# Layer 2 of a four-layer graph kernel: where its weights and sums are computed

## The chip, the cores and the metric

The kernel runs on one core of a Trainium2 chip. A core has five engines that run their own instruction streams side by side: TensorE (PE in the profile; its loads of stationary operands are PEld), VectorE (DVE), ScalarE (ACT), GpSimd (POOL) and SyncE (SP), which here issues the large loads. The metric is the device time of one execution in microseconds (us), the median of several runs.

## The reference

Four graph layers follow one another, each added to its input and normalised row by row. x has 4096 rows of 64 numbers, and adj is a 4096 x 4096 matrix of zeros and ones in f32 (64 MB), read by every layer. Layer 2 is the one that matters here:

```python
support = input @ weight
mask = (adj != 0).astype(support.dtype)
rank = jnp.cumsum(mask, axis=1)
deg = rank[:, -1:]
k = jnp.minimum(deg, float(MAX_NEIGH))      # MAX_NEIGH = 100
pos = rank - (deg - k)
w = mask * jnp.where(pos > 0, DECAY ** (k - pos), 0.0)   # DECAY = 0.5
out = w @ support + bias
```

Of each row's edges, the last one counts with weight 1, the one before it with 1/2, then 1/4, and so on. An edge's weight is therefore 2 to the power of minus the number of edges behind it in its row. Layers 1 and 3 are hyperbolic attention layers with a sum over all pairs of rows, and layer 0 is a mean over neighbours.

## The kernel before

**Tiling.** The rows i of adj are split into four groups s of 1024 (WW), worked on in the order 3, 2, 1, 0. The columns j are split into 32 blocks of 128, from the last to the first. One load (`load`, issued by SyncE) brings two blocks of one group, g = j // 2, as 1 MB of f32. The pool of loads has six buffers. Blocks lie on the partitions, rows i along the free dimension. The upper 16 bits of each f32 are read in place as bf16.

**Counting (`count`, matmul at L1569).** For every row the number of edges behind the current block is kept in PSUM, in a tile z that lives for the whole pass. Two matmuls per 512 rows bring it up to date for a block: `pass_by` times the edges of the previous block, then `enter` times the edges of this one. Afterwards z holds, for each j of the block and each row i, the number of edges behind j, less 255 if (j, i) is an edge. A z is thus counted into, read, and counted into again, block after block.

**Weights (`weights_of`, L1576).** ScalarE computes 2 to the power of minus (z + 282) from PSUM into a bf16 tile, with Exp: about nothing where there is no edge. A factor of 2 to the 27 is put back with the bias (L1494).

**Sums (`add_up`, L1581).** The supports are held as a sum of two f16 halves, high and low, in `halves[:, j]`, 128 columns wide. Four matmuls per group and block multiply the high and the low 64 columns with the two times 512 rows of weights. The two row halves go to the upper and the lower 64 partitions of one accumulator, so two such matmuls, each 64 columns wide, lie side by side in the array.

**Passes.** Groups 3 and 2 go together through the *wide pass*: z tiles of 128 x 1024, two of them. Groups 1 and 0 each have a *narrow pass*, in which the two z tiles are the two halves of 512 rows. Sums run one block behind the weights (`lag`). At the end of a pass ScalarE copies the accumulator (L1610), and `end_2` turns it back to rows with four transposes (L1095).

**Row work.** Normalising, preparing layer 3 and finishing layer 1 are written as generators that `tick` steps forward between blocks: small operations on VectorE and GpSimd, some casts, copies and logarithms on ScalarE, transposes on TensorE. In the wide pass the supports of the lower groups must be ready before their blocks come (`need`), and the pass pauses for them.

**Order.** Inside the layer-2 section `manual_schedule(engines=FIXED)` holds TensorE and ScalarE to the order in which the code is written. A planner orders VectorE's instructions. VectorE also holds, for every odd g, a check that adj contains only zeros and ones (`check`, L838): one instruction over the whole 1 MB load, which needs that load and nothing else. Layer 3 follows outside that section, and three of its sigmoids (L1074) were placed by the planner inside the last narrow pass, where ScalarE changes its function table before and after each.

Lines that the prediction names: L1569 counts; L1576 weights; L1581 sums; L838 check; L1080, L1082, L1077 the pair work of layers 1 and 3; L1494 to L1504 the first row work after a pass, L896 the product y that the casts L899 to L901 wait for; L947 copies, L950 logarithms of `prepare`.

Of the kernel before, what the change touches and what calls it, by code (L numbers as in the profile page):

```python
# [10 lines left out]
F32 = mybir.dt.float32  # L11
F16 = mybir.dt.float16
I32 = mybir.dt.int32
BF16 = mybir.dt.bfloat16
AF = mybir.ActivationFunctionType
ALU = mybir.AluOpType
# [3 lines left out]
P = 128  # L20
N = 4096
D = 64
NB = N // P
W = 512
NS = N // W
SB = W // P
# [3 lines left out]
WW = 1024  # L30
# [20 lines left out]
LN2 = 0.6931471805599453  # L51
OFF_EDGE = 255.0
CUT = 27.0
SUP = 512.0
SUP_TOP = 120.0

# [2 lines left out]
def gnn_stack_kernel(  # L59
# [15 lines left out]
    nc = tc.nc  # L75
    V = nc.vector
# [3 lines left out]
    ident = const.tile([P, P], F32, name="ident")  # L80
# [488 lines left out]
    def stream(fits):  # L569

        with ExitStack() as st:
# [69 lines left out]
            def need(tag):  # L641
                while tag not in done:
                    assert queues[0] or queues[1], tag
                    tick(1)
# [446 lines left out]
            def to_rows_of(sums):  # L1091

                t = take(F32, P, SB, 2, D)
                for k in range(SB):
                    nc.tensor.transpose(t[:, k], sums[:, k * P : (k + 1) * P], ident)  # L1095
                return t.rearrange("p k h f -> p h k f")
# [185 lines left out]
            enter = keep.tile([P, P], BF16, name="enter")  # L1282
            pass_by = keep.tile([P, P], BF16, name="pass_by")
            edge_of = keep.tile([P, P], BF16, name="edge_of")
            V.tensor_scalar(edge_of, ident, OFF_EDGE, None, ALU.mult)
            V.memset(pass_by, 1.0)
            nc.gpsimd.affine_select(
                out=enter, in_=pass_by, compare_op=ALU.is_gt, fill=0.0, base=0,
                pattern=[[-1, P]], channel_multiplier=1,
            )  # L1290
            V.tensor_sub(enter, enter, edge_of)
            V.tensor_sub(pass_by, pass_by, enter)
            at_edge = num(keep, "at_edge", 1)
            V.memset(at_edge, -(OFF_EDGE + CUT) * LN2)


            w2_twice = keep.tile([P, D], F32, name="w2_twice")
# [190 lines left out]
            def end_2(s, sums):  # L1488
                z = grp("z0")
                yield 1  # L1490
                yield from free()
                t = to_rows_of(sums)
                yield 1
                V.scalar_tensor_tensor(  # L1494
                    z.rearrange("p (h k) f -> p h k f", h=2)[:, 0], t[:, 0], 2.0**CUT / SUP,
                    b2_sb[:, None, :].to_broadcast([P, SB, D]), ALU.mult, ALU.add,
                )
                V.scalar_tensor_tensor(
                    z.rearrange("p (h k) f -> p h k f", h=2)[:, 1], t[:, 1], 2.0**CUT / SUP,
                    b2_sb[:, None, :].to_broadcast([P, SB, D]), ALU.mult, ALU.add,  # L1500
                )
                held.pop()
                yield 1
                V.tensor_add(z, z, x_of(2)[:, blocks(s), :])  # L1504
                yield 1
                yield from norm_rows(3, s, z, x2[:, blocks(s)])
                yield from prepare(3, s, att3, batt3_sb, curve3, 1e-30, good[:, 1], 40)

            def wide_pass(two):

                zs = [z_tile() for _ in two]

                accs = [ps.tile([P, W], F32, name="acc"), third_z[:, :W]]
                behind, lag = [None, None], []
                for g in reversed(range(NB // 2)):
                    edges = [load_2(s, g) for s in two]
                    need((2, 2 * g // WB))
                    for k in (1, 0):
                        j = 2 * g + k
                        w = sb.tile([P, 2, WW], F32, name="sq").bitcast(BF16)[:, :, :WW]  # L1520
                        for i, edge in enumerate(edges):
                            here = edge[:, k * WW : (k + 1) * WW]
                            count(zs[i], behind[i], here, j, WW)
                            behind[i] = here
                            weights_of(zs[i], WW, w[:, i])
                            if i == 1:
                                for of, acc in enumerate(accs if lag else ()):
                                    add_up(acc, *lag[of])
                                lag = [(j, w[:, n, :W], w[:, n, W:]) for n in range(2)]
                            if two[0] != GROUPS[0] or j < BLOCKS[4]:  # L1530
                                tick(1)
                for of, acc in enumerate(accs):
                    add_up(acc, *lag[of])
                return accs

            def narrow_pass(s):

                zs = [z_tile() for _ in range(2)]
                acc = ps.tile([P, W], F32, name="acc")
                behind, lag = [None, None], []  # L1540
                for g in reversed(range(NB // 2)):
                    edge = load_2(s, g)
                    for k in (1, 0):
                        j = 2 * g + k
                        w = sb.tile([P, 2, WW], F32, name="sq").bitcast(BF16)[:, 0, :WW]
                        for h in range(2):
                            here = edge[:, k * WW + h * W : k * WW + (h + 1) * W]
                            count(zs[h], behind[h], here, j, W)
                            behind[h] = here
                            weights_of(zs[h], W, w[:, h * W : (h + 1) * W])  # L1550
                        if lag:
                            add_up(acc, *lag.pop(0))
                        lag.append((j, w[:, :W], w[:, W:]))
                        tick(1)
                add_up(acc, *lag.pop(0))
                return [acc]

            def load_2(s, g):
                a, edge = load(s, g)
# [11 lines left out]
                                start=j == BLOCKS[0], stop=True, skip_group_check=True,  # L1571
                            )

            def weights_of(z, n, w):

                nc.scalar.activation(w, z[:, :n], AF.Exp, bias=at_edge, scale=-LN2)  # L1576

            def add_up(acc, j, *ws):
                for part in range(2):
                    for h, w in enumerate(ws):  # L1580
                        nc.tensor.matmul(  # L1581
                            acc[h * D : (h + 1) * D, :],
                            halves[:, j, part * D : (part + 1) * D], w,
                            start=j == BLOCKS[0] and part == 0,
                            stop=j == BLOCKS[-1] and part == 1,
                        )
# [16 lines left out]
            with tc.manual_schedule(engines=FIXED):  # L1603
                spare.append(of_third)

                for some in (GROUPS[:2], GROUPS[2:3], GROUPS[3:]):
                    accs = wide_pass(some) if len(some) == 2 else narrow_pass(some[0])
                    for s, acc in zip(some, accs):
                        sums = row.tile([P, W], F32, name="sums", bufs=2)
                        nc.scalar.copy(sums, acc)  # L1610
                        later(end_2(s, sums))
                spare_ends()

# [95 lines left out]
```

## Time and profile before

| | us |
|---|---|
| median of 3 runs | 1109.06 (1108.8 to 1110.59) |
| span of the profiled execution | 1106.6 |
| own time of that execution beyond its span | not given by the page |
| layer 2, first to last count (L1569) | 514.3 to 757.5 |
| weights of layer 2 (L1576), ScalarE busy | 149.3 |
| TensorE, VectorE, ScalarE busy over the span | 1001.9, 915.5, 803.1 |
| mean of one check (L838) | 2.29 |

The profile records one execution. The span goes from its first to its last instruction; the time of the runs also holds what lies around it. A line of the timeline reads: start, duration, engine, line, operation, output <- input, partitions x elements, how many in a row, and in brackets how long the engine was idle before and what ended that. Durations of two matmuls in a row overlap, so the distance of starts is the better measure on TensorE. A line of the chain of waits names the piece of work that the end of the kernel hung on at that time. Windows give busy time by engine in a stretch. "out<-in" uses the program's tile names; an output "z" of L1581 is the second accumulator, which lies in the third z tile.

### The profile page before, as it was taken

What the parts mean: (1) busy time and instruction counts of PE and PEld (TensorE: products, weight loads), DVE (VectorE), ACT (ScalarE), POOL (GpSimd) and SP (SyncE); (2) the same over time, 40 slices, a digit from 0 to 9 for tenths busy, and PEclk for the clock granted to TensorE, in tenths of its full rate; (3) what the DMA queues carried; (4) which work ended last, traced back from release to release, by engine and by line L of the source; (5) the groups of instructions that cost most, each with busy time, mean ns of one, the idle gap of its engine ahead of it and who ended that gap; (6) DMA issues with size and microseconds to landing.
All of it is one profiled execution on the core that took longest, in us unless ns stands there. A gap on an engine that the chain in (4) does not pass through costs nothing.

```text
span 1106.6 us, 13832 instructions
## 1 busy us (share of the span) xinstructions
PE 1001.9 (91%) x4949; PEld 392.4 (35%) x4949; DVE 915.5 (83%) x1452; ACT 803.1 (73%) x892; POOL 273.1 (25%) x649
## 2 busy tenths in 40 slices
PE   4998998889999999998998998789899999999980
PEld 2454554333333333332333332223333333333320
DVE  5777977989999999999456484545999999999996
ACT  0003123879999999897676788889899998998960
POOL 0011212010144443525500010000001444346173
PEclk8999999889999999999998999799999999999995
DMA  9999999536565565654877987477545656666400
GB/s 341 378 419 380 370 423 396 190 131 244 191 240 219 188 238 219 228 194 148 333 304 275 362 289 261 155 270 285 203 169 211 251 214 229 228 227 227 164 1 23
DMA packets 38581, 271.63 MB, mean 245 GB/s; under 512 B 4710, under 2 KB 4710, under 8 KB 5734
## 3 DMA queue, kind: packets, MB, share of 16 engines
q1 hardware_dynamic: 37728, 270.03, 64.8%
q8 instruction: 41, 0.67, 0.2%
q10 hardware_dynamic: 774, 0.63, 0.2%
q14 instruction: 38, 0.31, 0.1%
HBM read 269.58 MB, written 1.05 MB: 245 GB/s over the span
## 4 chain that ended last, share of the span: by engine, by line
PE 55%; DVE 24%; ACT 9%; DMA 5%; POOL 3%; issue 2%; ACTq 0%; SPq 0%; POOLq 0%; DVEq 0%
PE acc L1037 15%; PE z L1569 9%; DVE t L1082 7%; PE z L1059 7%; PE z L1065 6%; PE z L1062 6%; DVE t L1080 6%; DMA edges<-in_adj_dram 4%; PE acc L1581 3%; PE acc L1414 3%; ACT sq L1077 3%; ACT sq L1576 2%; DVE junk L838 2%; ACT sig L1074 1%; PE z L1581 1%
## 5 line engine op out<-in xcount | busy, mean ns | idle before, releaser
L1080 DVE SCALAR_TENSOR_TENSOR t<-z,sig 128x1024 f32<-128x1024 f32 x256 | 308.8, 1217 | 13.0 <-ACT sq L1077 6.8
L1077 ACT ACTIVATE sq<-z,turn 128x1024 f32<-128x1024 f32 x256 | 277.8, 1111 | 45.1 <-PE z L1065 18.4
L1082 DVE SCALAR_TENSOR_TENSOR t<-sq,t 128x2048 f32<-128x2048 f32 x128 | 297.3, 2322 | 0.5
L1074 ACT ACTIVATE sig<-left_b,right 128x1024 f32<-128x1024 f32 x256 | 285.9, 1146 | 1.9 <-DVE t L1080 1.3
L1037 PE MATMUL acc<-t,xe 128*64 128x512 f32 x1024 | 255.2, 608 | 17.2 <-DVE t L1082 16.8
L1059 PE MATMUL z<-edges,two_i 128*128 128x512 bf16 x512 | 201.2, 393 | 7.4 <-DVE t L1080 7.4
L1065 PE MATMUL z<-dst,src 74*128 74x512 f16 x512 | 195.5, 382 | 0.0
L1062 PE MATMUL z<-lo_hi,hi_lo 128*128 128x512 f16 x512 | 194.4, 380 | 0.0
L1576 ACT ACTIVATE sq<-z,at_edge 128x512 bf16<-128x512 f32 (+1 forms) x192 | 149.3, 828 | 46.0 <-PE z L1569 43.5
L838 DVE SCALAR_TENSOR_TENSOR t<-edges 128x2048 bf16<-128x2048 f32 x32 | 73.0, 2287 | 54.2 <-DMA edges<-in_adj_dram 54.2
L1037 PEld LDWEIGHTS acc<-t,xe 128*64 128x64 f32 x1024 | 63.8, 136 | 145.6 <-issue 83.8
L1569 PE MATMUL z<-edges,pass_by 128*128 128x512 bf16 x248 | 89.5, 401 | 17.9 <-ACT sq L1576 17.8
L1414 PE MATMUL acc<-edges,first 128*128 128x512 bf16 x256 | 80.1, 394 | 17.6 <-DMA edges<-in_adj_dram 17.3
L1059 PEld LDWEIGHTS <-two_i 128*128 128x128 bf16 x512 | 50.3, 98 | 128.9 <-issue 82.3
L1569 PE MATMUL z<-edges,enter 128*128 128x512 bf16 x256 | 91.0, 398 | 0.0
L1414 PE MATMUL acc<-edges,third 128*65 128x512 bf16 x256 | 80.0, 394 | 0.0
L838 DVE SCALAR_TENSOR_TENSOR junk<-edges 128x2048 bf16<-128x2048 f32 x32 | 73.1, 2286 | 4.7 <-DMA edges<-in_adj_dram 4.4
L1065 PEld LDWEIGHTS <-src 74*128 74x128 f16 x512 | 49.2, 96 | 70.5 <-issue 8.0
L1062 PEld LDWEIGHTS <-hi_lo 128*128 128x128 f16 x512 | 50.4, 98 | 57.1 <-issue 11.7
L1581 PE MATMUL acc<-sq,halves 128*64 128x512 bf16 x384 | 62.5, 403 | 1.0 <-ACT sums L1088 0.8
L869 POOL TENSOR_TENSOR sq<-z 128x512 f32<-128x512 f32 x8 | 14.2, 1776 | 164.3 <-DVE z L868 132.2
L1133 POOL TENSOR_TENSOR w_att<-x,u 128x512 f32<-128x512 f32 x6 | 15.6, 2595 | 141.2 <-ACT u L1128 141.2
(375 smaller groups left out, 940.9 us busy)
## 6 DMA issues: line engine op xcount, KB each, us to landing
edges<-in_adj_dram SPq DMA_DIRECT2D x256, 1024.0 KB, 4.7
x<-in_x_dram SPq DMA_DIRECT2D x4, 256.0 KB
out_dram<-x ACTq DMA_DIRECT2D x2, 256.0 KB
out_dram<-x SPq DMA_DIRECT2D x2, 256.0 KB
w_sb<-in_L_gnn_W_dram ACTq DMA_DIRECT2D x1, 32.0 KB, 4.8
w_twice<-in_L_gnn_weight_dram ACTq DMA_DIRECT2D x2, 16.0 KB, 8.6
given<-in_L_gnn_b_dram ACTq DMA_DIRECT2D x1, 0.2 KB
given<-in_L_gnn_bias_dram ACTq DMA_DIRECT2D x1, 0.2 KB
```

Of the source, the lines that this page charges most:

```text
L838: V.scalar_tensor_tensor(junk, a, 0.0, a, ALU.not_equal, ALU.not_equal, accum_out=odd[:, n : n + 1])
L1037: it = nc.tensor.matmul(acc[h * D : (h + 1) * D, :], xe[:, j, :], t[:, k, h * W : (h + 1) * W], start=j == BLOCKS[0], stop=j == BLOCKS[-1],)
L1059: nc.tensor.matmul(half, two_i, edge[:, at : at + W], start=True, stop=False)
L1062: nc.tensor.matmul(half, hi_lo[:, of], lo_hi[:, to], start=False, stop=False)
L1065: last = nc.tensor.matmul(half, src[:, of], dst[:, to], start=False, stop=True)
L1074: nc.scalar.activation(sig, left_b, AF.Sigmoid, bias=right[:, j : j + 1])
L1077: nc.scalar.activation(sq[:, k], zp, AF.Square, bias=turn, scale=-1.0 / UNIT)
L1080: V.scalar_tensor_tensor(t[:, k], zp, 0.0, sig, ALU.max, ALU.mult)
L1082: V.scalar_tensor_tensor(t, sq, HIGH**2, t, ALU.add, ALU.mult)
L1414: nc.tensor.matmul(accs[h][:m], lhs[:, j, :], edge[:, at : at + W], start=j == BLOCKS[0], stop=j == BLOCKS[-1],)
L1569: nc.tensor.matmul(z[:, h : h + W], lhs, rhs[:, h : h + W], start=j == BLOCKS[0], stop=True, skip_group_check=True,)
L1576: nc.scalar.activation(w, z[:, :n], AF.Exp, bias=at_edge, scale=-LN2)
```

## The change

Four things change in layer 2.

1. *The sign and scale of z.* The count matrices are multiplied by -128, so that z holds -128 times what it held. ScalarE's Exp takes the other scale.
2. *Weights as bit patterns.* A bf16 number that is a power of two has its exponent in bits 7 and up. VectorE adds a constant to z, cuts at 0 and writes int16, which is the bf16 weight itself. It does this for the second group (wide) or second half (narrow) wherever g is even, that is for a quarter of all weights; ScalarE does the rest.
3. *Wide pass:* the weights of two blocks share one tile, and their sums are made together, after the counts of the first block of the next g.
4. *Narrow passes:* each half has its own accumulator of 128 partitions, and one matmul with all 128 columns of `halves` adds the high and the low part at once (64 partitions each). Two copies at the end, and eight matmuls with `stack` (two stacked identities) that add high and low while turning to rows.

```diff
-            V.tensor_scalar(edge_of, ident, OFF_EDGE, None, ALU.mult)
-            V.memset(pass_by, 1.0)
+            V.tensor_scalar(edge_of, ident, OFF_EDGE * STEP, None, ALU.mult)
+            V.memset(pass_by, -STEP)
...
+            stack = keep.tile([P, D], F32, name="stack")
+            V.tensor_add(stack, ident[:, :D], ident[:, D:])
...
-                t = to_rows_of(sums)
+                if len(sums) == 1:
+                    t = to_rows_of(sums[0])
+                else:
+                    t = take(F32, P, SB, 2, D)
+                    for k in range(SB):
+                        for h, of in enumerate(sums):
+                            nc.tensor.matmul(
+                                t[:, k, h], of[:, k * P : (k + 1) * P], stack,
+                                start=True, stop=True,
+                            )
+                    t = t.rearrange("p k h f -> p h k f")
...
+                    w = sb.tile([P, 2, WW], F32, name="sq").bitcast(BF16)
                     for k in (1, 0):
                         j = 2 * g + k
-                        w = sb.tile([P, 2, WW], F32, name="sq").bitcast(BF16)[:, :, :WW]
                         for i, edge in enumerate(edges):
                             here = edge[:, k * WW : (k + 1) * WW]
                             count(zs[i], behind[i], here, j, WW)
                             behind[i] = here
-                            weights_of(zs[i], WW, w[:, i])
-                            if i == 1:
-                                for of, acc in enumerate(accs if lag else ()):
-                                    add_up(acc, *lag[of])
-                                lag = [(j, w[:, n, :W], w[:, n, W:]) for n in range(2)]
+                            weights_of(
+                                zs[i], WW, w[:, i, k * WW : (k + 1) * WW], i == 1 and g % 2 == 0
+                            )
                             if two[0] != GROUPS[0] or j < BLOCKS[4]:
                                 tick(1)
-                for of, acc in enumerate(accs):
-                    add_up(acc, *lag[of])
-                return accs
+                        if k == 1:
+                            for args in lag:
+                                add_up(*args)
+                            lag = []
+                    lag = [
+                        (
+                            accs[i], 2 * g + k,
+                            w[:, i, k * WW : k * WW + W], w[:, i, k * WW + W : (k + 1) * WW],
+                        )
+                        for k in (1, 0)
+                        for i in range(2)
+                    ]
+                for args in lag:
+                    add_up(*args)
+                return [[acc] for acc in accs]
...
-                acc = ps.tile([P, W], F32, name="acc")
-                behind, lag = [None, None], []
+                accs = [ps.tile([P, W], F32, name="acc"), third_z[:, :W]]
+                behind, lag = [None, None], [None, None]
+
+                def add(h):
+                    if lag[h] is not None:
+                        j, w = lag[h]
+                        nc.tensor.matmul(
+                            accs[h], halves[:, j, :], w,
+                            start=j == BLOCKS[0], stop=j == BLOCKS[-1],
+                        )
...
-                            weights_of(zs[h], W, w[:, h * W : (h + 1) * W])
-                        if lag:
-                            add_up(acc, *lag.pop(0))
-                        lag.append((j, w[:, :W], w[:, W:]))
+                            add(h)
+                            part = w[:, h * W : (h + 1) * W]
+                            weights_of(zs[h], W, part, h == 1 and g % 2 == 0)
+                            lag[h] = (j, part)
                         tick(1)
-                add_up(acc, *lag.pop(0))
-                return [acc]
+                for h in range(2):
+                    add(h)
+                return [accs]
...
-            def weights_of(z, n, w):
-
-                nc.scalar.activation(w, z[:, :n], AF.Exp, bias=at_edge, scale=-LN2)
+            def weights_of(z, n, w, as_bits):
+
+                if as_bits:
+                    V.tensor_scalar(
+                        w.bitcast(I16), z[:, :n], STEP * (BIAS - CUT - OFF_EDGE), 0.0,
+                        ALU.add, ALU.max,
+                    )
+                else:
+                    nc.scalar.activation(
+                        w, z[:, :n], AF.Exp, bias=at_edge, scale=LN2 / STEP
+                    )
...
-                    for s, acc in zip(some, accs):
-                        sums = row.tile([P, W], F32, name="sums", bufs=2)
-                        nc.scalar.copy(sums, acc)
+                    for s, of in zip(some, accs):
+                        sums = [row.tile([P, W], F32, name="sums", bufs=2) for _ in of]
+                        for to, acc in zip(sums, of):
+                            nc.scalar.copy(to, acc)
```

More of the change, by code (lines that the diff above doesn't have):

```diff
@@ L13 @@
 I32 = mybir.dt.int32
+I16 = mybir.dt.int16
 BF16 = mybir.dt.bfloat16
@@ L53 @@
 CUT = 27.0
+STEP = 128.0
+BIAS = 127.0
 SUP = 512.0
@@ L1290, in stream @@
             )
-            V.tensor_sub(enter, enter, edge_of)
+            V.tensor_add(enter, enter, edge_of)
             V.tensor_sub(pass_by, pass_by, enter)
```

## The prediction

> **What bounds the kernel now.** I began with busy time and the table of 40 slices: TensorE is busy for 91% of the span, but that is an average over four layers. The groups place the only code that changes, the counts (L1569), weights (L1576) and sums (L1581) of layer 2, between 514 and 760 us. So I asked for busy time by stage: the steady part of the wide pass, then the two narrow passes (columns: window, length, busy time of PE, PEld, DVE, ACT, POOL, clock, DMA share, GB/s).
>
> ```profile
> PE 1001.9 (91%) x4949; PEld 392.4 (35%) x4949; DVE 915.5 (83%) x1452; ACT 803.1 (73%) x892; POOL 273.1 (25%) x649
> ...
> 526.00:565.00 39.00, 39.00 (x218) 14.23 (x215) 15.60 (x17) 27.54 (x26) 14.17 (x38) 1.00 0.91 345
> ...
> 626.00:687.00 61.00, 55.78 (x312) 18.65 (x310) 43.42 (x141) 49.45 (x79) 6.59 (x16) 0.97 0.80 293
> 687.00:760.00 73.00, 60.66 (x343) 20.21 (x340) 29.20 (x89) 65.18 (x94) 2.39 (x8) 0.91 0.64 233
> ```
>
> In the wide pass TensorE never pauses, ScalarE idles 30%, VectorE 60%. In the narrow passes TensorE and ScalarE take turns, and in the first one VectorE is 71% busy. Next, TensorE in order of time, wide pass:
>
> ```profile
> 529.08 0.62 PE L1569 MATMUL z<-edges,pass_by 128*128 128x512 bf16 x2
> 529.54 0.61 PE L1569 MATMUL z<-edges,enter 128*128 128x512 bf16 x2
> 530.00 0.61 PE L1569 MATMUL z<-edges,pass_by 128*128 128x512 bf16 x2
> 530.45 0.61 PE L1569 MATMUL z<-edges,enter 128*128 128x512 bf16 x2
> 531.00 0.62 PE L1581 MATMUL acc<-sq,halves 128*64 128x512 bf16 x4
> 531.45 0.60 PE L1581 MATMUL z<-sq,halves 128*64 128x512 bf16 x4
> 531.98 0.62 PE L1569 MATMUL z<-edges,pass_by 128*128 128x512 bf16 x2
> ```
>
> One block lasts 2.90 us: four pairs of count matmuls at 0.455 (1.82), then eight sums in two groups (0.91), with 0.09 lost where counts turn into sums and 0.08 on the way back. The third view is ScalarE's timeline, with the two places where TensorE waits for it:
>
> ```profile
> 518.29 2.12 ACT L1576 ACTIVATE sq<-z,at_edge 128x1024 bf16<-128x1024 f32 x2
> ...
> 530.26 2.12 ACT L1576 ACTIVATE sq<-z,at_edge 128x1024 bf16<-128x1024 f32 x2 [0.78 <-PE z L1569]
> ...
> 738.41 1.27 ACT L1576 ACTIVATE sq<-z,at_edge 128x512 bf16<-128x512 f32 x2
> 739.87 1.27 ACT L1576 ACTIVATE sq<-z,at_edge 128x512 bf16<-128x512 f32 x2 [0.19 <-PE z L1569]
> ```
> ```profile
> 519.46 0.61 PE L1569 MATMUL z<-edges,pass_by 128*128 128x512 bf16 x2 [0.57 <-ACT sq L1576]
> ...
> 739.16 0.39 PE L1569 MATMUL z<-edges,pass_by 128*128 128x512 bf16 x1 [0.97 <-ACT sq L1576]
> ```
>
> They give the chain that each running count z imposes, since it is counted into, read, and counted into again. Wide: count start to weights start 1.18 (529.08 to 530.26), weights start to next count 1.17 (518.29 to 519.46), together 2.35 us. Before, 2.90 of TensorE work lay around that chain, so it never showed. Narrow: 0.75 (738.41 to 739.16) plus 0.71 (to 739.87), 1.46, against a block of 1.56 (counts start at 632.59, then 634.15). Last, the chain of waits in the first narrow pass:
>
> ```profile
> 634.64 2.21 DVE t L838 x2
> ...
> 645.48 1.46 DVE y L896
> ...
> 647.48 0.61 ACT ys L900
> ```
>
> From 629 to 649 the end hangs on VectorE: row work of groups 3 and 2, two checks of 2.2 us within it, and casts on ScalarE that wait for y.
>
> [...]VectorE stood 6.79 us before the check at 560.57, which waited for its transfer, and nothing passed it.
>
> **The change, part by part.**
>
> *Two blocks' sums at once (wide).* Per load pair (two blocks, two groups) TensorE's order becomes counts, 16 sums, counts. It saves one pair of mode changes, 0.17. But the second block's counts are now followed directly by the next load pair's, with only 1.82 of work where z's chain needs 2.35. New period: counts and sums 1.82 + 1.82 + 0.17 = 3.81, plus 2.35, is 6.16. The second group's z comes back 1.18 + 2.17 (518.29 to its count at 520.46) = 3.35 after the count began, and is wanted at 2.35 + 0.91 = 3.26: 0.09 more. So 6.25 against 5.80, +0.45 each. Of 15 hand-overs, the first lies in layer 1's tail and two (at 566 and 593) in pauses for the supports: 12 x 0.45 = 5.4, less 3 x 0.17 where only the saving stays: **+4.9**. The 2 bf16 blocks now share one "sq" buffer; its reader is done a period before it is rewritten, so no wait there. Loads: 2.1 MB in 6.25 us is 336 GB/s, less than the 345 now carried.
>
> *Weights on VectorE.* Taken from ScalarE: 16 of 64 in the wide pass, 16 of 64 in each narrow one. No row of before has the operation. Bounds: 1.217 for L1080 (128x1024 from PSUM) and, between it and 0.42 of L1494 (256 wide), 0.69 for 512;[...] the lower end is ScalarE's 1.06 and 0.63. I take 1.2 and 0.69, 0.60 in a dense queue. In the wide pass it buys nothing: z of the first group stays on ScalarE and sets the chain. What is queued behind and ahead is the cost: the checks (2.29 us, one per transfer) and row work share VectorE's queue, and TensorE waits for this weight at the next count. In the wide pass the first check of a pair lands ahead of the weight that could follow it, the second about when that weight is ready (540.24, against a ready time of 539.6); placed ahead it costs 0.8 per two load pairs, 6 in all; placed behind, nothing. I take +1.
>
> *First narrow pass.* The VectorE stretch from 629 to 649 takes in six weights of 0.60, one of them in the 1.15 wait for GpSimd: **+3**, and TensorE's saving there is lost. The other 20 blocks: next item -2, and a weight behind row work (0.16 to 0.7 each) or a check, 10 x 0.3 = +3; with ScalarE's relief (below) -2: **+2** in all.
>
> *Full-width sums (narrow).* Four half-width sums and two mode changes (0.56 + 0.08) become two matmuls at 0.23, so TensorE's work is 0.94 + 0.46 = 1.40, and the chain of 1.46 takes over: -0.10 a block.
>
> *Second narrow pass.* Some 26 blocks at -0.10; six at its start stay bound by ScalarE, where three early sigmoids bring two table loads of 1.28 each. Relief: a ScalarE job (casts, copies, logarithms, sigmoids) between two blocks is 0.63 shorter wherever VectorE has the second half; some 24 such jobs in both passes, half of them in such blocks, part of it covered by transposes on TensorE: between 0 and -7, I take -2 and -3. Late weights, VectorE being 40% busy: +1.5. Together -2.6 - 3 + 1.5: **-4**.
>
> *Ends.* Each narrow group now has two copies of 0.58 instead of one, and eight small matmuls instead of four transposes of 0.16: +0.6 per group: **+1.2**. The new constants are a few operations before layer 0, under its loads[...].
>
> Sum: 4.9 + 1 + 2 - 4 + 1.2 = **+5.1 us**. The profiled execution's span is 1106.6, so 1111.7; the median of the runs is 1109.06, 2.5 above the span for what lies around it, so **1114.2**.
>
> **Rivals.** (1) *VectorE's order becomes the bound.* If the planner puts checks or row work ahead of weights wherever both are near, 48 weights at 0.5 to 0.8 late cost +24 to +38, less what is now counted (5): about 1133. For it: four checks in the narrow passes waited 1.7 to 9.6 us for a transfer with the queue shut behind them. Against: a check that lands while an odd load is worked on, as at 715.51 and 739.89, meets no VectorE weight, since only even loads have them. (2) *Faster.* Mechanism: ScalarE's relief in the narrow passes, at its full -7, with -6 from the full-width sums and VectorE never late: -13 + 1.2 + 4.9 = -7, about 1102. It decides once late weights cost less than 0.1 us a block. Against: the VectorE stretch at 629 to 649. (3) *A draw.* The narrow gains cancel the wide loss: relief as taken, late weights nothing outside that stretch: 1109. (4) That the wide stall is absent since sums still cover it: the written order excludes it, as ScalarE and TensorE are held to it there.
>
> **How the numbers follow.** Likeliest case, 1111.4 to 1120: 0.48. Rival 1, from 1120 on: 0.21. Rival 2: 0.17. Rival 3 (and 4 with it): 0.14. Within 0.2%, 2.2 us, a measurement can't be told from no change. So slower 0.69, same 0.14, faster 0.17. The range 1103 to 1129 leaves out about half of rival 1 and a third of rival 2.
>
> **What would show it.** Wide pass: TensorE pauses of about 0.5 us before every second first-group count, released by the weights on ScalarE, and load pairs 6.2 apart. If they stay 5.8 or fall to 5.63, my largest term is wrong. Narrow: blocks of 1.46 with one sum after each count; casts of group 3 starting some 3 us later after the wide pass's end than now; waits of TensorE for the VectorE weights, small against 20 us. Large ones mean rival 1; none, with ScalarE idle, rival 2.

## The result and the profile after

The changed kernel takes 1117.67 us (median of 4 runs, 1115.37 to 1119.26), the kernel before 1108.93 (4 runs, the three above and one more, 1107.51 to 1110.59): a ratio of 1.0078, 95% interval 1.0056 to 1.0101, so 8.7 us slower. The profiled execution took 1115.37 us, its span is 1113.6. Up to layer 2 it runs like the one of before: ScalarE's first weight starts at 518.34 us, for 518.29.

First the busy time on the page of the changed kernel, then its busy time by stage: the same steady stretch of the wide pass, and the two narrow passes, each from about the end of the pass before (columns: window, length, busy PE, PEld, DVE, ACT, POOL, clock, DMA share, GB/s).

```profile
PE 992.4 (89%) x4845; PEld 404.9 (36%) x4845; DVE 954.4 (86%) x1501; ACT 771.9 (69%) x846; POOL 274.0 (25%) x649
```
```profile
526.00:565.00 39.00, 35.09 (x196) 13.63 (x194) 21.85 (x23) 19.60 (x18) 14.20 (x38) 1.00 0.85 305
635.00:698.00 63.00, 50.47 (x248) 22.16 (x247) 52.88 (x158) 43.87 (x65) 9.30 (x16) 1.00 0.83 291
698.00:765.00 67.00, 54.97 (x289) 25.34 (x289) 39.11 (x100) 55.04 (x79) 3.23 (x8) 0.95 0.69 237
```

In the wide pass TensorE had been busy without a break, 39.00 of 39.00; now it stands for 3.9 us. ScalarE's 27.54 fell to 19.60 and VectorE's 15.60 rose to 21.85. In the first narrow pass VectorE is busy 84% of the time. The work moved as planned, off ScalarE, which is busy 31 us less over the span (771.9, for 803.1). The time did not follow.

TensorE in order of time, one load pair of the wide pass after (start, duration, line, operation, and in brackets the wait before it and its releaser; sums are left out between):

```profile
543.88 0.61 PE L1604 MATMUL z<-edges,pass_by 128*128 128x512 bf16 x2
544.34 0.61 PE L1604 MATMUL z<-edges,enter 128*128 128x512 bf16 x2
545.36 0.61 PE L1604 MATMUL z<-edges,pass_by 128*128 128x512 bf16 x2 [0.41 <-DVE sq L1612]
...
548.20 0.63 PE L1604 MATMUL z<-edges,pass_by 128*128 128x512 bf16 x2
...
550.48 0.61 PE L1604 MATMUL z<-edges,pass_by 128*128 128x512 bf16 x2 [0.30 <-ACT sq L1617]
```

The sums no longer lie between 548.20 and 550.48, and the chain of one z shows: 2.28 us from count to count. The profile lists 0.30 us of that as idle; by the starts TensorE loses 0.45, as the last pair of counts starts at 549.57, and 0.455 is the usual distance. Load pairs without a late VectorE weight start 6.13 us apart (550.48, 556.61), where two blocks had taken 5.80.

TensorE's waits over the wide pass, first two lines of before (514 to 628 us), then the changed kernel's (514 to 632 us) and those of both its narrow passes (632 to 770 us): sum, times, longest.

```profile
PE aux L1258 <- POOL x_hl L1253: 3.7, 2, 2.6
...
PE z L1569 <- ACT sq L1576: 1.3, 2, 0.7
```

```profile
PE aux L1261 <- POOL x_hl L1256: 7.3, 2, 6.2
PE z L1604 <- ACT sq L1617: 4.1, 13, 0.6
PE z L1604 <- DVE sq L1612: 2.6, 4, 1.5
...
PE z L1604 <- ACT sq L1617: 15.1, 10, 4.4
PE z L1604 <- DVE sq L1612: 6.8, 8, 1.9
PE z L1570 <- DVE z L1513: 1.1, 1, 1.1
```

In the wide pass there are the chain's 4.1 us, VectorE's late weights 2.6, and a third wait that the prediction's sum has no term for. It lies in the second pause for the supports, and its longest part grew from 2.6 to 6.2 us. ScalarE's timeline, of before and then of the changed kernel, tells what was late there:

```profile
592.58 2.12 ACT L1576 ACTIVATE sq<-z,at_edge 128x1024 bf16<-128x1024 f32 x2 [0.78 <-PE z L1569]
594.58 0.62 ACT L1252 CAST x_hl<-x 128x512 f16<-128x512 f32 x1
...
601.57 1.11 ACT L1576 ACTIVATE sq<-z,at_edge 128x1024 bf16<-128x1024 f32 x1 [1.18 <-PE z L1569]
```

```profile
596.44 1.11 ACT L1617 ACTIVATE sq<-z,at_edge 128x1024 bf16<-128x1024 f32 x1 [2.69 <-PE z L1604]
601.58 0.62 ACT L1255 CAST x_hl<-x 128x512 f16<-128x512 f32 x1 [4.02 <-DVE x L1221]
...
608.46 1.11 ACT L1617 ACTIVATE sq<-z,at_edge 128x1024 bf16<-128x1024 f32 x1 [1.18 <-PE z L1604]
```

The cast that feeds the supports waits 4.02 us for x, layer 1's last row result on VectorE. Before, the same cast did not wait. Between the two pauses VectorE now has four weights of 1.2 us (at 581.44, 585.09, 594.24, 597.94) within that row work. Two checks moved as well: before, they started behind x (591.44 and 593.65), and now they stand ahead of it (591.95 and 595.45). The operation that writes x starts at 600.79, for 590.83 before. Of these 10 us the cast waits 4; before, ScalarE came to the cast only 3 us after x was ready. The pause, measured between ScalarE's weights for the first group on either side, is 12.0 us after and 9.0 before.

By stage: the wide pass ends 8.75 us later than before (last copy of its first group's sums at 634.26 against 625.51); the first narrow pass takes 63.2 us against 61.3, the second 67.4 against 73.5 (each from one pass's last copy to the next). This boundary is not the same in both. One of layer 3's three early sigmoids now stands, with its table load, between the two copies that end the first narrow pass:

```profile
695.05 0.59 ACT L1654 COPY sums<-acc 128x512 f32<-128x512 f32 x1 [0.26 <-PE acc L1570]
695.66 1.28 ACT L1077 ACT_TABLE_LOAD   x1
696.95 1.15 ACT L1077 ACTIVATE sig<-left_b,right 128x1024 f32<-128x1024 f32 x1
698.01 0.57 ACT L1654 COPY sums<-z 128x512 f32<-128x512 f32 x1
```

Before, all three come after the pass's copy (687.35; the first table load is at 689.12). If these 2.4 us are counted with the second pass as before, the first takes 60.8 us and the second 69.8, which is -0.5 and -3.7. At the end of the second pass the loss is down to 4.6; what follows brings it to 7.0 in this execution.

### The profile page after: what moved, and what is told of

It reads as the page before. It is cut to its first block, busy times and chain, and to the rows that moved or that the text cites. A ratio compares the mean times of both kernels' runs of the same rounds, so it can differ in the third digit from the quotient of the medians.

```text
span 1113.6 us, 13643 instructions
## 1 busy us (share of the span) xinstructions
PE 992.4 (89%) x4845; PEld 404.9 (36%) x4845; DVE 954.4 (86%) x1501; ACT 771.9 (69%) x846; POOL 274.0 (25%) x649
## 5 line engine op out<-in xcount | busy, mean ns | idle before, releaser
L1080 ACT ACTIVATE sq<-z,turn 128x1024 f32<-128x1024 f32 x256 | 277.9, 1111 | 46.2 <-PE z L1068 19.7
L1617 ACT ACTIVATE sq<-z,at_edge 128x512 bf16<-128x512 f32 (+1 forms) x144 | 116.3, 830 | 76.4 <-PE z L1604 67.7
L1612 DVE TENSOR_SCALAR sq<-z 128x512 int16<-128x512 f32 (+1 forms) x48 | 41.6, 866 | 25.6 <-PE z L1604 17.3
```

The lines of the kernel that those rows point to most:

```text
L1080: nc.scalar.activation(sq[:, k], zp, AF.Square, bias=turn, scale=-1.0 / UNIT)
```

## The experiments

The change has three parts: A, the sums of two blocks at once in the wide pass; B, a quarter of the weights on VectorE; C, the full-width sums in the narrow passes with their two copies and the matmuls with "stack". The twelve kernels are combinations of these; two of them, e6 and e12, change the tile of the row work as well. All twelve keep the new sign and scale of z. e2, e7 and e11 have A, the others the old order of sums in the wide pass. The times below are ratios to the kernel before with their 95% intervals; a difference in microseconds is a difference of ratios times 1109, and its interval combines the two.

| run | parts | median us | ratio to before |
|---|---|---|---|
| the change | A, B, C | 1117.67 | 1.0078 (1.0056 to 1.0101) |
| e1_no_batch | B, C | 1115.57 | 1.0057 (1.0037 to 1.0076) |
| e2_no_bits | A, C | 1113.77 | 1.0040 (1.0019 to 1.0061) |
| e3_full_only | C | 1107.57 | 0.9977 (0.9960 to 0.9994) |
| e4_narrow_bits_full | C, B in both narrow passes | 1113.95 | 1.0038 (1.0020 to 1.0056) |
| e5_second_pass_bits | C, B in the second narrow pass | 1106.04 | 0.9975 (0.9959 to 0.9991) |
| e6_rows_out_of_third | e4, row work in "aux" only | 1111.19 | 1.0021 (0.9998 to 1.0043) |
| e7_batch_only | A | 1114.67 | 1.0043 (1.0028 to 1.0059) |
| e8_second_pass_bits_only | B in the second narrow pass | 1107.28 | 0.9975 (0.9957 to 0.9993) |
| e9_wide_all | e5 and B in the wide pass | 1107.79 | 0.9998 (0.9975 to 1.0021) |
| e10_wide_some | e9, not between the pauses | 1105.01 | 0.9963 (0.9941 to 0.9985) |
| e11_batch_again | e10 and A | 1112.55 | 1.0023 (1.0003 to 1.0042) |
| e12_rows_in_aux | e10, row work in "aux" only | 1104.66 | 0.9958 (0.9938 to 0.9979) |

### The batching

e1 gives the wide pass its old order of sums and keeps VectorE's weights; e7 has the batching alone; e2 has it beside C; e11 on the fastest kernel. The edit of e1 (e7, e2 and e11 are the same lines, kept):

```diff
...
-                        if k == 1:
-                            for args in lag:
-                                add_up(*args)
-                            lag = []
-                    lag = [(accs[i], 2 * g + k, ...) for k in (1, 0) for i in range(2)]
+                            if i == 1:
+                                for of, acc in enumerate(accs if lag else ()):
+                                    add_up(acc, *lag[of])
+                                lag = [(j, w[:, n, :W], w[:, n, W:]) for n in range(2)]
...
```

> The wide pass takes its sums once per block again, as before; VectorE keeps its weights and the narrow passes their full-width sums. My theory (the chain of a count shows where no sums lie around it): the 0.30 us that TensorE waits at every second first-group count goes, and the slack hides the four waits for VectorE in the wide pass too; what stays is VectorE's delay of layer 1's last rows (about +3), narrow passes +3.3 and -8.0, and the ends. 1111 to 1113, against 1117.7 with all parts and 1108.9 before. Rival (VectorE's order is the bound, whatever order the sums have): 1116 to 1118, with the wait for x before the second supports pause unchanged and the wide pass still 7 us or more longer than before.

> Of the change only the sums of two blocks at once in the wide pass. Theory (each of 12 hand-overs from one load pair to the next leaves the chain of z open by 0.30 to 0.45 us): +3 to +5, 1112 to 1114, load pairs 6.13 us apart, and the two narrow passes as before. Rival (the pauses for the supports and the throttle take it up): within 1 us of before, 1108 to 1110.

> ScalarE makes all weights; the sums of two blocks at once (wide) and the full-width sums (narrow) stay. My theory: the wide pass keeps +4 to +5 (0.30 to 0.45 us at each of 12 hand-overs), the wait for x before the second supports pause returns to what it was before, the first narrow pass loses VectorE's late weights and the second loses the relief of ScalarE (-3): 1110 to 1113. Rival (VectorE's weights do most of the harm): 1107 to 1109. Rival (relief by VectorE is the only gain there is): 1115 or more, with the second narrow pass no shorter than before.

The edit of e2 leaves every weight to ScalarE:

```diff
-    weights_of(zs[i], WW, ..., i == 1 and g % 2 == 0)
+    weights_of(zs[i], WW, ..., False)
-    weights_of(zs[h], W, part, h == 1 and g % 2 == 0)
+    weights_of(zs[h], W, part, False)
```

Batching alone costs 4.8 us (3.1 to 6.5), of an expected 3 to 5; beside C it costs 7.0 ± 3.0 (e2 less e3), and e2 lies between its two expectations. TensorE's timeline of e7:

```profile
540.13 0.61 PE L1594 MATMUL z<-edges,pass_by 128*128 128x512 bf16 x2 [0.30 <-ACT sq L1607]
...
543.97 0.62 PE L1594 MATMUL z<-edges,pass_by 128*128 128x512 bf16 x2
...
546.25 0.61 PE L1594 MATMUL z<-edges,pass_by 128*128 128x512 bf16 x2 [0.30 <-ACT sq L1607]
```

The same 0.30 stands there with ScalarE making every weight, and the pairs are 6.12 us apart. Of the steady stretch from 526 to 565 us the trace of before lists no wait of TensorE, nor does e1's list a wait for a weight. So the wait comes with the order of the sums, not with VectorE.

How much of the wide pass it takes can be read from ScalarE's timelines, from its first weight to the first copy of the sums: 107.2 us before, 111.0 with the batching alone (e7), 111.0 with VectorE's weights but not the batching (e1), and 115.9 in the change. The two parts add 3.7 and 3.8 of the 8.7. What e7 has beyond its 3.7 does not lie in the wide pass. Its narrow passes, with the code of before, took 64.7 and 75.4 us in place of 61.3 and 73.5, at a granted clock of 0.92 and 0.86 in place of 0.97 and 0.91; "as before", as expected, they were not.

e1 itself missed: 1115.6, between the two expectations, and the batching was worth only 2.3 ± 3.3 there. I put this down to the row work of the first narrow pass, which the later end of the wide pass meets in a better place, and e11 was to test it:

> Sums of two blocks at once in the wide pass, put on top of the fastest kernel so far (full-width sums in the narrow passes; VectorE's weights in the second narrow pass and in the wide pass outside the stretch between the supports pauses; 1105.0 without the batching). Theory (batching costs +5 to +6 by itself, and it cost only 2.1 on top of all other parts because it moved the row work of the first narrow pass to a better place): 1110 to 1112. Rival 1 (batching costs little once VectorE has a share of the weights): 1106 to 1108. Rival 2 (with batching TensorE has no slack left for VectorE's late weights, so the two together cost more than their sum): 1113 or more.

It took 6.7 ± 3.2 us more than e10, so with the weights gone from the first narrow pass the batching costs about its own price again. The first rival, that batching is cheap once VectorE has a share, falls. That its cost in the full change was smaller agrees with the stall of 4.6 us in that pass (below, present in e1, 1.1 in the change). But e11, which has no VectorE weight in that pass, has this stall too, 3.1 us against 0.8 in e10: the batching can move it either way. The intervals are too wide to call the theory shown.

### VectorE's weights in the narrow passes

> Of the change only the full-width sums of the narrow passes, with their two copies and eight small matmuls per group; the wide pass and the weights are as before. My theory: blocks of 1.46 in place of 1.56 us for some 40 blocks not bound by VectorE or ScalarE, about -4, and +1.2 to +2 for the ends: 1106 to 1107.5. Rival (the block stays bound by ScalarE, one weight of 0.63 us for each half and its hand-overs, so the sums were hidden anyway): no gain, 1109 to 1111.

> The wide pass as before; in the narrow passes full-width sums and VectorE's quarter of the weights. My theory: first narrow pass +2 to +3, second -8, ends +1.5: 1104.5 to 1107, faster than before and no slower than the full-width sums alone. Rival (VectorE's order is the bound): its weights cost more in the first narrow pass than they give in the second, 1108 to 1111.

> Wide pass as before, full-width sums in both narrow passes, VectorE's weights in the second narrow pass only. My theory now: VectorE's weights cost in the first narrow pass (68.3 us with them, 59.5 without, from the wide pass's last copy of its sums to the narrow one's) because row work and checks stand ahead of them there, and pay in the second (67.7 against 74.8): first pass 59 to 60, second 67 to 68, so 7 less than full-width sums alone, some 1101 to 1103. Rival (the second pass was shorter only because the first one had pushed the row work out of it): first pass 59.5, second 73 to 75, 1107 to 1109.

> Of the change only VectorE's weights in the second narrow pass; sums half-width and as before. Theory (the gain there is ScalarE's relief, and the sums' form has nothing to do with it): second pass 67 to 70 us against 73.5, 1102 to 1106. Rival (relief shows only where the block is 1.46 long, not 1.56): second pass above 71.5, 1107 to 1109.

e4 is C with the line of `narrow_pass` as in the change; e3 has `False` there; e5 and e8 (e8 without C) have

```diff
-    weights_of(zs[h], W, part, h == 1 and g % 2 == 0)
+    weights_of(zs[h], W, part, h == 1 and g % 2 == 0 and s == GROUPS[3])
```

The full-width sums give 2.6 us (0.7 to 4.4), about as expected. VectorE's weights in the first narrow pass, the only difference of e4 and e5, cost 7.0 ± 2.7: my expectation of e4, faster than before, was wrong, and the rival's 1108 to 1111 too low.

In the second pass they shorten the pass itself, by 6.0 us beside full-width sums (74.8 to 68.8; e3, e5) but by 2.1 without them (73.5 to 71.4; before, e8). The whole time follows less: e5 and e3 differ by 0.2 ± 2.6, and e5 missed its 1101 to 1103. e8 is 2.8 us (0.8 to 4.8) faster than before. Its time fell where the rival had it, its pass within 0.1 us of that; so the profiles speak for the rival, that the relief shows in full only beside the shorter block. Here the busy time of the two narrow passes in e4, then the second one in e3 and in e5, one stage view of each kernel:

```profile
627.82:696.08 68.26, 53.11 (x243) 23.11 (x247) 53.15 (x157) 44.19 (x66) 8.06 (x16) 0.95 0.76 271
696.08:763.74 67.66, 55.22 (x285) 25.50 (x289) 39.52 (x102) 55.26 (x79) 3.34 (x8) 0.95 0.69 239
```
```profile
685.97:760.76 74.79, 59.31 (x286) 26.52 (x289) 29.00 (x86) 66.96 (x98) 2.72 (x8) 0.86 0.67 232
```
```profile
684.96:753.79 68.83, 56.42 (x286) 25.50 (x289) 39.16 (x102) 57.64 (x82) 5.23 (x8) 0.90 0.71 246
```

ScalarE is busy 66.96 of 74.79 us without VectorE's help and 57.64 of 68.83 with it; TensorE's clock is higher too (0.86, 0.90). The fall of the second pass in the change thus takes both parts: C alone lengthens the pass by 1.3 us (e3), B alone shortens it by 2.1 (e8), both shorten it by 4.6 (e5, against before).

How much of this reaches the end is open. The timed runs of e3 and e5 say 0.2 ± 2.6. Their profiled spans differ by 4.9, but e3's is that of an execution 1.7 us above its median, e5's of one 1.6 below. Some of it is lost after the pass: from the last copy to the end of the span the kernels with half-width sums take 345.7 to 345.9 us (before, e7, e8), those with full-width sums and ScalarE's weights 346.8 and 347.1 (e3, e2), and the nine with VectorE's weights in the second pass as well 347.8 to 350.5. Why these take longer there is not shown.

The first narrow pass of e4 takes 68.3 us, e3's 59.5. Of the difference 2.4 us are only moved: in e4, as in e1, e6 and the change, an early sigmoid with its table load stands ahead of the pass's last copy, in e3 and e5 behind it. TensorE's waits of e4, then of e6, from 626 to 700 us:

```profile
PE z L1594 <- ACT sq L1607: 7.4, 5, 4.2
PE z L1594 <- DVE sq L1602: 5.0, 4, 1.5
PE z L1560 <- DVE z L1513: 4.6, 1, 4.6
```
```profile
PE z L1594 <- ACT sq L1607: 10.4, 5, 4.4
PE z L1594 <- DVE sq L1602: 5.0, 6, 1.4
```

The third line of e4 is not among the waits of before, and no weight is in it. L1560 is a sum into the left half of the third z tile (`accs[1]`); L1513 is row work that reads that tile's right half. VectorE's timeline of e4 shows why the reader was late:

```profile
641.27 0.69 DVE L1602 TENSOR_SCALAR sq<-z 128x512 int16<-128x512 f32 x1
...
643.27 0.69 DVE L880 TENSOR_TENSOR x<-z,n_r 128x512 f32<-128x512 f32 x1
...
643.95 2.28 DVE L841 SCALAR_TENSOR_TENSOR t<-edges 128x2048 bf16<-128x2048 f32 x1
...
646.71 0.41 DVE L1513 SCALAR_TENSOR_TENSOR z<-z,given_b 128x256 f32<-128x256 f32 x1
```

Four weights (the first at 632.20, the last at 641.27) delay the chain of small row operations, a check of 2.28 us then lands ahead of L1513, and TensorE's next instruction is the sum that waits until 647.17. In e3, L1513 starts at 640.19, ahead of the check, and the wait is 0.9 us. e6 keeps the row work out of that tile during the narrow passes:

```diff
+                    if len(some) == 1:
+                        spare.clear()
                     accs = wide_pass(some) if len(some) == 2 else narrow_pass(some[0])
```

> As with full-width sums and VectorE's weights in both narrow passes and the wide pass as before (1113.95), but the row work is kept out of the third z tile while the narrow passes run: it takes the one 'aux' tile each time. Theory: TensorE's longest wait there, 4.6 us before a sum into the third z tile for row work in that tile's other half (DVE z), is a loss of its own: it goes, the first narrow pass is 3 to 5 us shorter, and in all it is 1109 to 1111. Rival (the row work's turn, not its tile, is late: VectorE is behind by the same amount and the next weight inherits the wait): the wait moves to sq or to the weights and the pass stays at 66 to 69 us, 1113 to 1115; or the row work, now with one tile, is later by more: 1115 or above.

The wait is gone from the list and the first pass takes 65.1 us in place of 68.3, as expected; in the timed runs the gain is 1.9 ± 3.2, so it is the trace that shows it. Part of the wait was inherited, as the rival had it: within the pass, the waits for ScalarE's weights rise from 3.2 to 5.5 us. Of what is left, 65.1 against e3's 59.5, the moved sigmoid is 2.4; for the other 3.2 stands VectorE's order, as TensorE waits 5.0 us for VectorE's weights there, which e3 does not have. e12 does the same on the fastest kernel, which has only 0.8 us of that wait:

> The same fastest kernel, without the batching, and with the row work kept out of the third z tile during the narrow passes. Theory: TensorE's waits before sums into that tile (0.9 and some of 0.2 us) go, 0 to 2 us less: 1103 to 1105. Rival: with one tile for its transposes the row work is later, ScalarE's and VectorE's work bunches up, and the narrow passes are 1 to 4 us longer: 1106 to 1109.

1104.66 against 1105.01: the expected value, but no difference that these runs can tell.

### VectorE's weights in the wide pass

> Full-width sums in both narrow passes, VectorE's weights in the second narrow pass (1106.0 with these two) and in the whole wide pass, whose sums are taken per block as before. Theory: four weights of 1.2 us between the two supports pauses stand in layer 1's last row work, x is ready some 4 us later, the second pause (the gap between weights on ScalarE across it) is 13 us long in place of 9.0; the earlier part of the pass is some 2 us shorter: 1107 to 1109. Rival (the slack of the per-block order hides all of it): pause of 9 us, 1104 to 1106.

> The same, but between the two supports pauses (the load pairs 6 and 4) ScalarE makes the wide pass's weights. Theory: the second pause is 9 us again, and the relief before the first pause stays: 2 to 4 us less than with VectorE's weights in the whole wide pass, 1103 to 1106. Rival (what delays x is not these four weights but where the earlier ones have put the row work): pause still 12 to 13 us, no difference between the two kernels.

Both have the old order of sums and B in the second narrow pass. The edit of e10 to e9:

```diff
-    weights_of(zs[i], WW, w[:, i], i == 1 and g % 2 == 0)
+    weights_of(zs[i], WW, w[:, i], i == 1 and g % 2 == 0 and g not in (4, 6))
```

ScalarE's timeline around the second pause, of e9 and then of e10:

```profile
588.04 1.11 ACT L1607 ACTIVATE sq<-z,at_edge 128x1024 bf16<-128x1024 f32 x1 [1.78 <-PE z L1594]
594.14 0.62 ACT L1255 CAST x_hl<-x 128x512 f16<-128x512 f32 x1 [4.99 <-DVE x L1221]
...
601.02 1.11 ACT L1607 ACTIVATE sq<-z,at_edge 128x1024 bf16<-128x1024 f32 x1 [1.18 <-PE z L1594]
```
```profile
592.73 2.12 ACT L1607 ACTIVATE sq<-z,at_edge 128x1024 bf16<-128x1024 f32 x2 [0.78 <-PE z L1594]
594.74 0.62 ACT L1255 CAST x_hl<-x 128x512 f16<-128x512 f32 x1
...
602.66 1.11 ACT L1607 ACTIVATE sq<-z,at_edge 128x1024 bf16<-128x1024 f32 x1 [1.18 <-PE z L1594]
```

With the four weights the cast waits 4.99 us for x and the pause is 13.0 us; without them it doesn't wait and the pause is 9.9, where 13 and 9 were expected. The whole time is 3.9 ± 3.5 less. In e10 the two checks stand behind x again (592.12 and 594.33), in e9 ahead of it (585.05 and 588.54). So the four weights within layer 1's last row work, and the two checks that come ahead of x with them, are what the second pause grew by. Outside that stretch these runs show no harm from VectorE's weights in the wide pass under the old order of sums (e10 against e5: 1.3 ± 3.0 less). e10 and e12 beat both kernels: 4.1 and 4.7 us less than the one before (0.9963 and 0.9958).

## Why the prediction was right, and where its terms were not

It said 1114.2 us, 1103 to 1129, slower 0.69; measured 1117.7. The direction and the range hold, the named case too (1111.4 to 1120). The sum was +5.1 and is +8.7, and its terms were off in both directions. In the profiled execution the wide pass gives +8.7 for a predicted +5.9, the two narrow passes together -4.1 for -2, and what follows +2.4 for +1.2: +7.0 for +5.1. The rest of the +8.7 lies between single executions and medians. The 2.5 us put on top of the span for what lies around it were too many as well: each run takes 1.7 to 1.9 us more than its span.

**Two blocks' sums at once, +4.9.** Right in mechanism. That the size agrees, 4.8 alone (3.1 to 6.5), is in part luck. The chain is 2.28 and not 2.35 us, and a load pair grew by 0.33 to 6.13, not by 0.45 to 6.25. Twelve hand-overs at 0.33, less the 0.5 that is saved elsewhere, make 3.4, and e7's wide pass grew by 3.7. What the prediction calls a mode change is 0.09 and 0.10 us in the trace of the change: the last counts and the first sums start 0.54 apart (545.81, 546.35), where 0.455 is usual between pairs of counts, and the last sums and the next counts 0.53 (547.67, 548.20), where 0.43 lies between two groups of four half-width sums. The full-width sums of the narrow passes, of the counts' form 128*128, start 0.23 after a count and 0.21 before the next (655.14, 655.37, 655.58). What TensorE does in the 0.09 and 0.10 us is not shown. The rest of e7's time stands in passes whose code did not change. Beside other parts the batching costs up to 7.0 ± 3.0; where the rest arises I leave open, but for one stretch at half clock in e2 (last section).

**Wide weights late, +1 (0 to +6).** This term was the furthest off in the change. One weight takes what was estimated, 1.23 us (at 632.84) or 0.69 (at 639.37), and 0.60 from the start of that one to the next operation. The weights themselves were late by 2.6 us in four waits, as the step describes: a weight at 541.70 stood behind checks at 537.10 and 539.49. The larger part was missing. I had noted that row work shares VectorE's queue and had asked only what it does to the weights. What the weights do to the row work was in no term: x is written 10 us later, and the cast waits 4 of them. By themselves the weights lengthen the wide pass by 3.8 us (e1) or 4.0 (e9). With the batching's 3.7 this accounts for about 7.5 of the 8.7 us; the remainder I leave open.

**First narrow pass, +2.** It came out as +1.9 in the change, but not by the terms given, so the agreement is luck: 2.4 us are the sigmoid, without which it is -0.5. By its own working the weights cost +4 there (+3 in the stretch, +3 outside, -2 relief) and the full-width sums gave 2. Measured one at a time, the weights cost 7.0 ± 2.7. About 3 us of that, in the trace, is a wait that I had not looked for: the change puts the second accumulator into a tile whose other half the row work uses. The rest fits VectorE's order, which is rival 1's mechanism in one stretch. In the full change the stall was only 1.1.

**Full-width sums and ends.** For C alone the steps say -2, -2.6 and +1.2, in all -3.4; measured -2.6 (-4.4 to -0.7). The block of 1.46 is there (1.45), but only the first pass got shorter, by 1.8 us; the second of e3 is 1.3 longer than before: TensorE's waits for ScalarE's weights in it are no less (13.1 us, 12.3 before), and its clock is lower (0.86, 0.91 before). The ends were sized right up to layer 3's first sum: from the last copy of the sums to it took 7.85 us before and takes 9.04 now.

**Second narrow pass, -4.** With the sigmoid counted as before, the pass fell by 3.7 us. What stood for it, -2.6 from the sums and -3 from ScalarE's relief, was wrong: the sums alone give nothing there, and the relief gives 2.1 alone and 6.0 beside them.

**Rivals.** Rival 1 had the right place, VectorE's order, and too high a price: TensorE waits 9.4 us for VectorE's weights in all three passes (2.6 and 6.8), where it needed 24. Rival 2 needs the relief without late weights; e10 comes nearest to it, 4 us faster than before, by taking VectorE's weights out of the two stretches where row work is due and leaving out the batching. Rival 4, no wide stall, is excluded by the 13 waits.

## What to carry to other kernels

Before sums, copies or other filler are moved out of a loop, work out the longest chain from a buffer's write to its next write: the filler may be what covers it, and here less than half a microsecond open at each of some 12 hand-overs made the wide pass 3.7 us longer. Work given to a less busy engine is paid where that engine's queue holds something the end waits for, so price it against what comes after it in each stage, not only for its own delay; one choice by stage (the second narrow pass yes, the first no, between the pauses no), with the sums left in their old order in the wide pass, turned a loss of 8.7 us into a gain of 4.1. And when an accumulator moves into a shared tile, list the tile's other readers.

## What of the hardware was not expected

TensorE's clock. In the kernel before, counts start 0.42 us apart at 701.75 and 702.17, where 0.23 is usual: TensorE runs at half rate there. A pause of TensorE and the granted clock around it, in the same kernel (third number from the end):

```profile
701.36 0.58 PE L1569 MATMUL z<-edges,pass_by 128*128 128x512 bf16 x1 [3.30 <-ACT sq L1576]
```
```profile
698.00:700.00 2.00, 0.07 (x2) 0.09 (x1) 1.73 (x9) 1.97 (x3) 0.00 (x0) 0.98 0.51 213
700.00:702.00 2.00, 0.64 (x2) 0.25 (x2) 1.93 (x4) 1.97 (x4) 0.00 (x0) 0.50 0.00 0
...
708.00:710.00 2.00, 2.00 (x13) 0.99 (x13) 0.00 (x0) 0.89 (x2) 0.00 (x0) 0.50 0.04 8
710.00:712.00 2.00, 2.00 (x13) 0.71 (x11) 0.00 (x0) 1.19 (x3) 0.00 (x0) 0.96 0.13 29
```

The pause began at 698.06, and the clock was down from about 699.9 on (1.00 up to 699.5, 0.94 in the next half microsecond, then 0.50), after less than 2 us of it. In e3 it went down between 692 and 694 us (1.00 in the stretch before, 0.88 in this one, 0.50 in the next), with TensorE busy for 0.45 of the 2.00 us before 692 and for 1.52 of the 2.00 after. In the kernel before, TensorE then worked for 2.9 us (701.36 to 704.22) until it had to wait for ScalarE again, and the clock stayed at 0.50. That ended at about 710.2, some 3.8 us after TensorE had begun to work without a pause (706.40). How long a pause or a stretch of work it takes to change the clock is not shown.

Equal code need not meet it in the same place. e2 and e7 have the same wide pass, and in both TensorE is busy for 0.90 of the 2.00 us from 568 on, in the first pause for the supports. The clock fell there in e2 and did not in e7 (0.64 and 1.00 from 568 to 570 us, 0.50 and 1.00 from 570 to 572), and from ScalarE's first weight to the first copy e2's wide pass took 113.3 us, e7's 111.0.

Whole runs go with the clock too: of the 22 of e2, one at a clock of 0.957 took 1118.98 us and one at 0.972 took 1108.07. The mean clock is not what makes the change slower: its four runs have a mean clock of 0.965, the 53 runs of the kernel before that were taken beside e1 have 0.966. The repeated runs left intervals of some 2 us either way, so differences of under 3 us between two of these kernels are not told apart here.
